# One PSUM tile for both halves of a product, matmuls of 384 columns in the last state step, and another order of the products in the last two groups

## The chip, the cores and the metric

The kernel runs on one core of a Trainium2 chip. A time is the device time of one execution in microseconds. Three executions of the kernel before took 2102.91, 2104.47 and 2105.32 us; their median, 2104.47 us, is the time before. The profile is of one more execution.

Five engines run side by side: TensorE (PE), VectorE (DVE), ScalarE (ACT), GpSimd (POOL) and SyncE (SP, which issues the DMAs). Each takes its own instructions in order, and they wait for one another through semaphores.

## The reference

128 graphs of 128 nodes, each node with 256 features, go through two layers. The first has three steps of message passing with a gated state; the second is an attention over the edges.

```python
# layer 0, h = relu(layernorm(x)); three steps i = 0, 1, 2
m    = einsum('bnd,de->bne', h, weight[i])
aggr = einsum('bst,bsd->btd', A, m)            # A = adj != 0
gi, gh = aggr @ w_ih.T + b_ih, h @ w_hh.T + b_hh   # three gates of 256 each
r, z = sigmoid(i_r + h_r), sigmoid(i_z + h_z)
n    = tanh(i_n + r * h_n)
h    = (1 - z) * n + z * h
# x = x + h
# layer 1, h = relu(layernorm(x))
Wh    = h @ W;  s = Wh.sum(-1)
e     = where(adj == 0, -inf, leaky_relu(s[:, None] + s[None, :], 0.2))
x     = x + softmax(e, -1) @ Wh
```

All values are fp32. Nearly all the arithmetic is in `gi` and `gh`, for the three steps.

## The kernel before, in words

**Groups and steps.** The 128 graphs are worked on in 32 groups of four (G = 4), each with three steps, so there are 96 steps, followed by the group's attention. A table `turns` interleaves the steps of different groups: while one group is in step 0, another is in step 1 and a third in step 2. A step takes about 22 us (the span of 2100.6 us over 96), with its share of the rest.

**The gate products as seven.** The message weights are folded into w_ih, so each step multiplies the state (hT, weights s_hh) and the edge sums (aT, weights s_x0 to s_x2). Both the weights (2x2 blocks of 128) and the columns (two halves of 256) are split in two, and the product of the 2x2 blocks is done with seven block products in place of eight; the sums of halves it needs are hs and gs, made by POOL and DVE. The running sums are called X, Y and Q. In `products` (line 709) the order is: product 1 into X; X is copied to Y (`put`, ACT line 733 or 737 and 739); product 5 into Q; 6 into Y, and Y copied to T2 in SBUF; 7 into Y, Y copied to T3, and Q added to T3 (`add`, DVE line 743); 2 into X; 4 into Y; 3 into Q, and Q added to T2. At the end X, Y, T2 and T3 are the four blocks of the result, and the gates are computed from each.

**PSUM.** Each of X, Y and Q is two tiles: x_rz and x_n and so on, `[P, 2, H]` fp32 with H = 256, which is one bank of 512 values per partition each. [...] T2 and T3 in SBUF are pairs in the same way (t2_rz, t2_n, t3_rz, t3_n).

**Steps 0 and 1** (`gru`) give a transposed result: the weights stand still, and 256 columns of the data stream by. The rz bank holds the gates r and z (four matmuls of 256 columns per product: two gates, state and edges), the n bank holds the state's and the edges' part of n apart (two matmuls of 256). Line 694 issues them.

**Step 2** (`gru_rows`) gives rows, one node per partition: the data stand still, and the weights stream by. Here the rz bank holds r and z for two graphs, filled per product with four matmuls of 256 columns (two graphs, state and edges); the n bank holds the state's and the edges' part of n for both graphs, filled with four matmuls of 128 columns. Line 701 issues them. The biases are laid into X and Q beforehand by a copy on ACT (`seed`, line 726). Per graph pair the gates are one tanh over r and z (ACT line 837, reading the rz bank) and two DVE operations with n (lines 841 and 846, reading the n bank).

**What sets the order.** Each operation is recorded in a `Plan` with an engine, a cost in ns, what it reads and writes (a buffer or a unit range of it), and for the seven products a due time; these form one chain on PE. `Plan.run` then lists all operations in the order in which they would start by these costs, and the instructions are written out in that order, under a scheduler that leaves the order alone. Semaphore waits are put in afterwards, from the order in which instructions touch a tile. Operations on the edges (line 621, bf16), transposes and the attention's products (650, 1077) fill the places between.

**The last two groups** have the same order of the seven products as all others; some of the attention's tiles there take over the banks of x, y and q (`late_bank`).

Of the kernel before, what the change touches and what calls it, by code (L numbers as in the profile page):

```python
# [17 lines left out]
G = 4  # L18
# [197 lines left out]
def kernel(  # L216
# [67 lines left out]
        "w1_sum": (1, "all", const, [P, D]),  # L284
    }
    DTYPE = {"at": I32, "a": BF16, "pl": U16, "plT": U16, "pe": U16, "peT": U16, "p3": BF16}
    phys = {}

    def make(tag, n, kind, pool, shape):
        for s in range(SETS if kind == "set" else 1):  # L290
            for k in range(n):
                phys[tag, s, k] = pool.tile(shape, DTYPE.get(tag, F32), name=f"{tag}_{s}{k}")
# [4 lines left out]
    def ap(b):  # L297
        return phys[(b.tag,) + b.slot]
# [41 lines left out]
    def nat(b):  # L340
        return plain(b)[:, :3 * KD * D].rearrange("p (c e) -> p c e", e=D)

    def turned(src, dst, evict):

        for a in range(2):
            for k in range(KD):
                ps = bank()

                def turn(k=k, a=a, ps=ps):
                    for c in range(3):  # L350
                        nc.tensor.transpose(flat(ps)[:, c * P:(c + 1) * P],
                                            nat(src)[:, 3 * a + c, k * P:(k + 1) * P], ident)
                op("PE", 330, turn, [(src, a, a + 1)], [ps])
                to_sbuf(evict[k % len(evict)], 3 * P, ps, dst[k], 3 * P * a)

# [24 lines left out]
    def weights():  # L380
# [47 lines left out]
        homes = [[buf("h1"), last("hT")] for _ in range(L)]  # L428
        for layer in range(L):
            if layer == 1:  # L430
                turned(w_hh_nat, w_hhT, ("DVE", "ACT"))
                block_sums(w_hhT, W["s_hh"], "POOL", 1000)
            wT, half, msg = uT[layer // 2], layer % 2, w_msg[layer]
            for e in range(KD):
# [38 lines left out]

        def seeds():
            nc.gpsimd.tensor_tensor(plain(tmp[0]), plain(tmp[0]), plain(tmp[1]), OP.add)
            for t, q in ((tmp[0], 0), (tmp[2], 2)):
                nc.gpsimd.tensor_copy(ap(W["seed_x"])[:, q:q + 2, :], halves(t, 0))
                nc.gpsimd.tensor_tensor(ap(W["seed_q"])[:, q:q + 2, :], halves(t, 1), halves(t, 0),
                                        OP.subtract)
        op("POOL", 4000, seeds, tmp, [W["seed_x"], W["seed_q"]] + tmp[:1])  # L480

# [190 lines left out]
    DATA = [None, 0, 2, 3, 7, 4, 6, 5]  # L672
    R, Z, NN = 0, 1, 2

    def product(bank, i, parts, first, rows=False):


        def unit(t, w):
            return (t, DATA[i], DATA[i] + 1) if DATA[i] < 4 else (w, DATA[i] - 4, DATA[i] - 3)

        def source(t, w):
            if DATA[i] < 4:
                return ap(t)[:, DATA[i] // 2, (DATA[i] % 2) * H:(DATA[i] % 2 + 1) * H]
            return ap(w)[:, DATA[i] - 4, :]

        todo = []
        for term in range(max(len(p) for _, p in parts)):
            todo.append([(half, q) + p[term] for half, (q, p) in enumerate(parts) if term < len(p)])
        if len(todo) == 1:
            todo = [[m] for m in todo[0]]  # L690
        for c, chunk in enumerate(todo):
            def mm(c=c, chunk=chunk):
                for m, (half, q, w, t, sums) in enumerate(chunk):
                    nc.tensor.matmul(ap(bank)[:, half, :], ap(w)[:, i - 1, q, :], source(t, sums),  # L694
                                     start=(first and c == 0 and m == 0), stop=False,
                                     skip_group_check=True)

            def mm_rows(chunk=chunk):
                half, q, w, t, sums = chunk[0]
                for m in range(2):  # L700
                    nc.tensor.matmul(  # L701
                        ap(bank)[:, m, half * P:(half + len(chunk)) * P],
                        source(t, sums)[:, m * N:(m + 1) * N],
                        ap(w)[:, i - 1, q:q + len(chunk), :].rearrange("p q m -> p (q m)"),
                        start=False, stop=False, skip_group_check=True)
            plan.cursor += 432 * len(chunk) * SLOT // GATES
            op("PE", 432 * len(chunk), mm_rows if rows else mm,
               [unit(t, s) for _, _, _, t, s in chunk] + [(w, i - 1, i) for _, _, w, _, _ in chunk],
               [bank], due=plan.cursor)

    def products(layer, hT, hs, aT, gs, rows=False):

        five, seven, three, four = (7, 5, 4, 3) if rows else (5, 7, 3, 4)
        state, edges = (W["s_hh"], hT, hs), (W[f"s_x{layer}"], aT, gs)
        kinds = (("rz", ((R, (state, edges)), (Z, (state, edges)))),  # L720
                 ("n", ((NN, (state,)), (NN, (edges,)))))
        X, Y, Q, T2, T3 = ({} for _ in range(5))

        def seed(b, kind, t):
            q = 0 if kind == "rz" else 2
            op("ACT", 590, lambda: nc.scalar.copy(
                ap(b), ap(t)[:, q:q + 2].rearrange("p (o q) m -> p o (q m)", o=1)
                .to_broadcast([P, 2, 2 * P])), [t], [b])

        def put(t, y, bias=None, mark=None):  # L730

            if bias is None or rows:
                op("ACT", 590, lambda: nc.scalar.copy(ap(t), ap(y)), [y], [t], mark=mark)  # L733
                return

            def halves():
                nc.scalar.activation(ap(t)[:, 0], ap(y)[:, 0], AF.Identity,
                                     bias=ap(W["bias_n"])[:, bias:bias + 1])
                nc.scalar.copy(ap(t)[:, 1], ap(y)[:, 1])
            op("ACT", 760, halves, [y, W["bias_n"]], [t], mark=mark)  # L740

        def add(t, q):
            op("DVE", 690, lambda: nc.vector.tensor_tensor(ap(t), ap(t), ap(q), OP.add), [q], [t])  # L743

        for kind, parts in kinds:
            X[kind], Y[kind] = buf("x_" + kind), buf("y_" + kind)
            if rows:
                seed(X[kind], kind, W["seed_x"])
            product(X[kind], 1, parts, not rows, rows=rows)
            put(Y[kind], X[kind], 1 if kind == "n" else None, mark=(plan.group, layer, kind))  # L750
        for kind, parts in kinds:
            Q[kind] = buf("q_" + kind)
            if rows:
                seed(Q[kind], kind, W["seed_q"])
            product(Q[kind], five, parts, not rows, rows=rows)
        for kind, parts in kinds:
            product(Y[kind], 6, parts, False, rows=rows)
            T2[kind] = buf("t2_" + kind)
            put(T2[kind], Y[kind], 2 if kind == "n" else None)
        for kind, parts in kinds:  # L760
            product(Y[kind], seven, parts, False, rows=rows)
            T3[kind] = buf("t3_" + kind)
            put(T3[kind], Y[kind])
            add(T3[kind], Q[kind])
        for kind, parts in kinds:
            product(X[kind], 2, parts, False, rows=rows)
        for kind, parts in kinds:
            product(Y[kind], four, parts, False, rows=rows)
        for kind, parts in kinds:
            product(Q[kind], three, parts, False, rows=rows)  # L770
            add(T2[kind], Q[kind])

        y, t2 = ((0, 1), (1, 0)) if rows else ((1, 0), (0, 1))
        return ((1, 1, T3), (0, 0, X), y + (Y,), t2 + (T2,)), X

# [48 lines left out]
    def gru_rows(layer, hT, hs, aT, gs, rows, x1):  # L826
# [6 lines left out]
        for j, n, src in blocks:  # L833
            i = 2 * n + j
            outs, graphs = slice(j * P, (j + 1) * P), slice(2 * n, 2 * n + 2)
            s_rz, nn = src["rz"], src["n"]
            op("ACT", 700, lambda outs=outs, graphs=graphs, s_rz=s_rz: nc.scalar.activation(
                ap(rz).rearrange("p q (g d) -> p g q d", g=G)[:, graphs, :, outs],
                ap(s_rz).rearrange("p g (q m) -> p g q m", q=2), AF.Tanh, scale=0.5),
               [s_rz], [(rz, i, i + 1), (rz, 4 + i, 5 + i)])  # L840
            op("DVE", 422, lambda outs=outs, graphs=graphs, nn=nn: nc.vector.scalar_tensor_tensor(
                view(u)[:, graphs, outs],
                ap(rz)[:, 0].rearrange("p (g d) -> p g d", g=G)[:, graphs, outs], 1.0,
                ap(nn)[:, :, 0:P], op0=OP.add, op1=OP.mult),
               [nn, (rz, i, i + 1)], [(u, i, i + 1)], two=nn.tag[0] == "t")
            op("DVE", 422, lambda outs=outs, graphs=graphs, nn=nn: nc.vector.scalar_tensor_tensor(
                view(u)[:, graphs, outs], view(u)[:, graphs, outs], 0.5, ap(nn)[:, :, P:2 * P],
                op0=OP.mult, op1=OP.add),
               [nn], [(u, i, i + 1)], two=nn.tag[0] == "t")
        for n in (1, 0):  # L850
            d, lo, hi = buf("d"), 2 * n, 2 * n + 2
            cols = slice(n * GN, (n + 1) * GN)
# [340 lines left out]
```

## Time and profile before

| what | value |
|---|---|
| median of three runs | 2104.47 us |
| the profiled execution | 2102.59 us, its span 2100.6 us |
| PE busy | 2086.8 us, 99% |
| DVE, ACT, POOL busy | 1668.5, 1592.4, 938.0 us |
| clock granted to PE | 1.0 of full |
| first 50 us | PE busy 45.02 us |
| last 21 us | PE busy 15.58 us |
| fp32 matmuls of 256 columns, steps 0 and 1 (line 694) | 2 records each, about 380 ns a record by itself |
| fp32 matmuls of step 2 (line 701) | 256 columns: about 380 ns a record; 128 columns: 275 ns |

[...] What a record costs in a stream is the distance from its start to the next one's start; the timeline shows that. A line of groups gives the operation, its tiles (numbers left out), count, busy time, mean of one, and the idle time of the engine before them with what ended most of it. A line of the timeline gives start, duration, engine, line and operation.

### The profile page before, as it was taken

How to read it: one execution, taken by the hardware profiler on the slowest of the kernel's cores; microseconds unless marked ns; L12 is line 12 of the kernel's file. 1: busy time of each engine (PE TensorE's matmuls, PEld its weight loads, DVE VectorE, ACT ScalarE, POOL GpSimd, SP SyncE). 2: the span in 40 equal slices, each digit the busy share in tenths (PEclk: the TensorE clock that was granted, in tenths of full speed). 3: DMA queues.
4: the chain of work that ended last, by engine and by line, in shares of the span. 5: the costliest groups of instructions: out<-in, count | busy, mean ns of one | idle time of the engine just before them, and what ended most of it. 6: DMA issues, size and time to landing. Idle time of an engine off the chain costs nothing.

```text
span 2100.6 us, 33940 instructions
## 1 busy us (share of the span) xinstructions
PE 2086.8 (99%) x12416; PEld 1862.0 (89%) x12416; DVE 1668.5 (79%) x3370; ACT 1592.4 (76%) x2849; POOL 938.0 (45%) x881
## 2 busy tenths in 40 slices
PE   9999999999999999999999999999999999999998
PEld 6888888898888998898988889988989888988887
DVE  7777888888877888877888778888778887778778
ACT  6577878777878777777778787777777787777676
POOL 5545454345443445544454434455444544335330
PEclk9999999999999999999999999999999999999999
DMA  4323223232233222233222332222322223222331
GB/s 131 61 51 56 53 49 81 61 59 63 69 74 76 57 60 64 68 81 66 52 65 68 73 76 56 61 64 69 80 66 57 60 64 78 56 51 51 76 76 36
DMA packets 365158, 137.21 MB, mean 65 GB/s; under 512 B 296384, under 2 KB 364736, under 8 KB 364992
## 3 DMA queue, kind: packets, MB, share of 16 engines
q1 hardware_dynamic: 364992, 135.05, 28.5%
q8 instruction: 97, 1.59, 0.3%
q14 instruction: 69, 0.57, 0.1%
HBM read 45.36 MB, written 16.78 MB: 30 GB/s over the span
## 4 chain that ended last, share of the span: by engine, by line
PE 97%; DVE 2%; ACT 1%; issue 0%; DMA 0%; DVEq 0%
PE y_rz L694 16%; PE q_rz L694 11%; PE x_rz L694 10%; PE y_n L694 8%; PE y_rz L701 8%; PE misc L621 6%; PE x_n L694 5%; PE q_n L694 5%; PE q_rz L701 5%; PE x_rz L701 5%; PE misc L1077 5%; PE y_n L701 4%; PE x_n L701 3%; PE q_n L701 3%; PE misc L650 2%; PE misc L450 0%
## 5 line engine op out<-in xcount | busy, mean ns | idle before, releaser
L578 POOL TENSOR_TENSOR r<-rows 128x512 f32<-128x512 f32 x126 | 136.1, 1100 | 268.0 <-ACT rows L561 183.4
L733 ACT COPY t_rz<-y_rz 128x512 f32<-128x512 f32 x192 | 112.4, 585 | 178.8 <-PE y_rz L694 89.5
L743 DVE TENSOR_TENSOR t_rz<-t_rz,q_rz 128x512 f32<-128x512 f32 x192 | 131.2, 684 | 98.0 <-ACT t_rz L733 57.0
L603 POOL TENSOR_TENSOR pl<-d,pl 128x512 bf16<-128x512 f32 x64 | 74.7, 1170 | 294.1 <-ACT pl L601 293.9
L694 PE MATMUL y_rz<-hs,s_hh 128*128 128x256 f32 x768 | 197.5, 380 | 0.0
L694 PE MATMUL y_rz<-gs,s_x 128*128 128x256 f32 x768 | 197.1, 379 | 0.0
L668 POOL TENSOR_TENSOR hs<-hT,hs 128x256 f32<-128x256 f32 x96 | 81.8, 852 | 241.6 <-PE q_n L701 173.7
L664 POOL TENSOR_TENSOR hs<-hT 128x512 f32<-128x512 f32 x96 | 130.4, 1358 | 100.4 <-ACT hT L561 32.1
L694 PEld LDWEIGHTS y_rz<-gs,s_x 128*128 128x128 f32 x768 | 145.9, 190 | 19.8
L694 PEld LDWEIGHTS y_rz<-hs,s_hh 128*128 128x128 f32 x768 | 143.1, 190 | 18.8 <-issue 0.5
L581 POOL TENSOR_TENSOR p<-r 128x512 bf16<-128x512 f32 x126 | 153.2, 1235 | 0.0
L743 DVE TENSOR_TENSOR t_n<-t_n,q_n 128x512 f32<-128x512 f32 x192 | 131.2, 683 | 20.5 <-ACT t_n L733 8.2
L694 PE MATMUL x_rz<-hT,s_hh 128*128 128x256 f32 x512 | 131.5, 379 | 0.0
L694 PE MATMUL x_rz<-aT,s_x 128*128 128x256 f32 x512 | 131.4, 379 | 0.0
L624 ACT COPY aT<-misc 128x512 f32<-128x512 f32 x190 | 110.5, 584 | 13.6 <-PE misc L621 9.6
L501 DVE BATCH_NORM_STATS2 st<-rows 128x6 f32<-128x256 f32 x128 | 45.1, 413 | 94.6 <-DMA rows<-in_x_dram 94.5
L816 DVE TENSOR_TENSOR d<-hT,u 128x512 f32<-128x512 f32 x128 | 110.6, 864 | 8.9 <-ACT u L813 8.7
L694 PE MATMUL y_n<-hs,s_hh 128*128 128x256 f32 x384 | 114.4, 379 | 0.0
L694 PE MATMUL y_n<-gs,s_x 128*128 128x256 f32 x384 | 114.2, 379 | 0.0
L598 POOL TENSOR_TENSOR d<-hT,pl 128x512 f32<-128x512 f32 x64 | 90.8, 1421 | 51.4 <-ACT pl L596 45.6
L1077 PE MATMUL misc<-w,uT 128*128 128x256 f32 x480 | 113.3, 380 | 0.3 <-ACT uT L655 0.3
L694 PEld LDWEIGHTS x_rz<-aT,s_x 128*128 128x128 f32 x512 | 97.2, 190 | 13.2
(277 smaller groups left out, 6500.6 us busy)
## 6 DMA issues: line engine op xcount, KB each, us to landing
rows<-in_x_dram SPq DMA_DIRECT2D x32, 512.0 KB, 4.2
x<-in_x_dram SPq DMA_DIRECT2D x32, 512.0 KB, 3.9
out_dram<-x SPq DMA_DIRECT2D x31, 512.0 KB, 2.9
at<-in_adj_dram SPq DMA_DIRECT2D x32, 256.0 KB, 2.8
plT<-pl SPq DMA_TRANSPOSE x186, 3.3
peT<-pe SPq DMA_TRANSPOSE x60, 3.1
e<-in_L_gnn_weight_dram SPq DMA_DIRECT2D x3, 256.0 KB, 3.2
rz<-in_L_gnn_w_ih_dram SPq DMA_DIRECT2D x2, 384.0 KB, 3.9
```

The source lines that it names most:

```text
L578: op("POOL", 1106, lambda part=part: nc.gpsimd.tensor_tensor(ap(r1)[:, part], ap(rows)[:, part], top(rows)[:, part], OP.subtract), [(rows, ...
L581: op("POOL", 1050, lambda part=part: nc.gpsimd.tensor_tensor(ap(p3)[:, part], ap(r1)[:, part], top(r1)[:, part], OP.subtract), [(r1, n, n ...
L598: op("POOL", 1150, lambda k=k, r=r: nc.gpsimd.tensor_tensor(ap(r), ap(hT)[:, k], part(pl, k, 0), OP.subtract), [(hT, 2 * k, 2 * k + 2), (p ...
L621: nc.tensor.matmul(flat(ps)[:, b * N:(b + 1) * N], part(i, b, k), ap(a)[:, b, :], start=(i == 0), stop=(i == 2))
L624: op("ACT", 590, lambda k=k, ps=ps: nc.scalar.copy(ap(dst)[:, k, :], flat(ps)), [ps], [(dst, 2 * k, 2 * k + 2)])
L664: op(eng, cost, lambda: sub(ap(w)[:, 0:2, :], blocks()[:, 1::2, :], blocks()[:, 0:2, :], OP.subtract), [t], [(w, 0, 2)], two=True)
L694: nc.tensor.matmul(ap(bank)[:, half, :], ap(w)[:, i - 1, q, :], source(t, sums), start=(first and c == 0 and m == 0), stop=False, skip_gro ...
L701: nc.tensor.matmul(ap(bank)[:, m, half * P:(half + len(chunk)) * P], source(t, sums)[:, m * N:(m + 1) * N], ap(w)[:, i - 1, q:q + len(chun ...
L733: op("ACT", 590, lambda: nc.scalar.copy(ap(t), ap(y)), [y], [t], mark=mark)
L743: op("DVE", 690, lambda: nc.vector.tensor_tensor(ap(t), ap(t), ap(q), OP.add), [q], [t])
L816: op("DVE", 690, lambda j=j, d=d, cols=cols: nc.vector.tensor_tensor(ap(d), ap(hT)[:, j, :], ap(u)[:, cols], OP.subtract), [(hT, lo, hi), ...
L1077: nc.tensor.matmul(ap(ps)[:, b, :], ap(uT)[:, k, (m + b) * N:(m + b + 1) * N], ap(w1)[:, k, :], start=(k == 0), stop=(k == KD - 1))
```

## The change

It has three parts.

First, `make` cuts the two halves of a pair from one tile: `both["x"]` is `[P, 2, 2, H]`, x_rz is its part 0 and x_n its part 1; likewise y, q, t2 and t3. In PSUM such a tile is two banks.

Second, in step 2 a bank now belongs to a graph. Its four blocks of 128 columns are: the state's part of n, r, z, the edges' part of n. The weights s_hh are laid out as n, r, z (by turning w_hh's blocks in another order), the weights s_x as r, z, n; so the state's product adds into columns 0 to 383 and the edges' product into columns 128 to 511, each with one matmul of 384 columns. The seeds are laid out in the same order. The gates of a graph pair read both banks at once.

Third, in the last two groups product 2 into X and 6 into Y come ahead of 5 and 7, and the gates of X ahead of those of T3.

```diff
     def make(tag, n, kind, pool, shape):
+        name, _, half = tag.partition("_")
+        if shape == [P, 2, H] and half:
+            if half == "rz":
+                both[name] = pool.tile([P, 2, 2, H], F32, name=name)
+            phys[tag, 0, 0] = both[name][:, ("rz", "n").index(half)]
+            return
...
-                turned(w_hh_nat, w_hhT, ("DVE", "ACT"))
+                turned(w_hh_nat, w_hhT, ("DVE", "ACT"), (4, 5, 0, 1, 2, 3))
...
-            def mm_rows(chunk=chunk):
-                half, q, w, t, sums = chunk[0]
-                for m in range(2):
-                    nc.tensor.matmul(
-                        ap(bank)[:, m, half * P:(half + len(chunk)) * P],
-                        source(t, sums)[:, m * N:(m + 1) * N],
-                        ap(w)[:, i - 1, q:q + len(chunk), :].rearrange("p q m -> p (q m)"),
-                        start=False, stop=False, skip_group_check=True)
...
+    def product_rows(bank, i, m, sources):
+        for c, (w, t, sums) in enumerate(sources):
+            plan.cursor += 645 * SLOT // GATES
+            op("PE", 645, lambda c=c, w=w, t=t, sums=sums: nc.tensor.matmul(
+                flat(bank)[:, c * P:(c + 3) * P], source(i, t, sums)[:, m * N:(m + 1) * N],
+                ap(w)[:, i - 1].rearrange("p q m -> p (q m)"), start=False, stop=False,
+                skip_group_check=True), [unit(i, t, sums), (w, i - 1, i)], [bank], due=plan.cursor)
...
-        def seed(b, kind, t):
-            q = 0 if kind == "rz" else 2
-            op("ACT", 590, lambda: nc.scalar.copy(
-                ap(b), ap(t)[:, q:q + 2].rearrange("p (o q) m -> p o (q m)", o=1)
-                .to_broadcast([P, 2, 2 * P])), [t], [b])
+        def seed(b, t):
+            op("ACT", 590, lambda: nc.scalar.copy(flat(b), plain(t)), [t], [b])
...
+        steps = {"Q5": q_five, "Y6": y_six, "Y7": y_seven, "X2": x_two, "Y4": y_four, "Q3": q_three}
+        order = ("Q5 Y6 Y7 X2 Y4 Q3" if plan.group < NG - 2 else "Y6 X2 Q5 Y7 Y4 Q3" if plan.group < NG - 1 else "Y6 X2 Q5 Y7 Y4 Q3").split()
+        for name in order:
+            for kind, parts in kinds:
+                steps[name](kind, parts)
+        x_first = order.index("X2") < order.index("Y7")
...
+            banks_of = [src["rz"], src["n"]]
+            sums = both[src["rz"].tag.split("_")[0]].rearrange("p g a m -> p g (a m)").rearrange(
+                "p g (q m) -> p g q m", q=4)
...
+            op("ACT", 700, lambda outs=outs, graphs=graphs, sums=sums: nc.scalar.activation(
+                ap(rz).rearrange("p q (g d) -> p g q d", g=G)[:, graphs, :, outs], sums[:, :, 1:3, :],
+                AF.Tanh, scale=0.5), banks_of, [(rz, i, i + 1), (rz, 4 + i, 5 + i)])
```

In the changed kernel the matmuls of steps 0 and 1 are at line 703, those of step 2 at line 717, the copies at 744 (seed), 749, 753 and 755, the add at 759, the tanh of the gates at 818 and 836 (steps 0 and 1) and 869 (step 2).

## The prediction

> **What bounds the kernel now.** I read the page first: share of each engine, then the chain that ended last.
>
> ```profile
> PE 2086.8 (99%) x12416; PEld 1862.0 (89%) x12416; DVE 1668.5 (79%) x3370; ACT 1592.4 (76%) x2849; POOL 938.0 (45%) x881
> ...
> PE 97%; DVE 2%; ACT 1%; issue 0%; DMA 0%; DVEq 0%
> ```
>
> TensorE is busy for 99% of the span and carries 97% of the chain. Since a busy PE need not be a PE at its peak, I next read the timeline in a steady stretch, for the distance between the starts of its groups:
>
> ```profile
> 1025.61 0.61 PE L701 MATMUL q_n<-s_hh,hs 128*128 128x128 f32 x4
> 1026.05 0.61 PE L701 MATMUL q_n<-s_x,gs 128*128 128x128 f32 x4
> 1026.50 1.03 PE L701 MATMUL y_rz<-s_hh,hs 128*128 128x256 f32 x4
> 1027.37 1.03 PE L701 MATMUL y_rz<-s_x,gs 128*128 128x256 f32 x4
> 1028.23 0.61 PE L701 MATMUL y_n<-s_hh,hs 128*128 128x128 f32 x4
> ```
>
> One fp32 matmul is two records here. Four records of 256 columns take 0.865 us from start to start (216 ns each), four of 128 columns 0.445 us (112 ns). Neither a reader nor a weight load opens a gap. Why none does is seen at one of the few places where PE stops, in the last 60 us, where its queue runs short:
>
> ```profile
> 2056.44 1.03 PE L701 MATMUL x_rz<-s_x,aT 128*128 128x256 f32 x4
> ...
> 2057.50 0.57 ACT L733 COPY y_rz<-x_rz 128x512 f32<-128x512 f32 x1 [0.73 <-PE x_rz L701]
> ...
> 2057.98 0.60 ACT L726 COPY q_rz<-seed_q 128x512 f32<-128x512 f32 x1
> ...
> 2058.63 1.13 PE L701 MATMUL q_rz<-s_hh,hs 128*128 128x256 f32 x4 [0.28 <-ACT q_rz L726]
> ```
>
> The last x_rz record has streamed in at 2056.44+0.865=2057.30. ACT starts 0.20 us later; PE starts 0.05 us after ACT's copy ends (2058.58), and its first group then takes 1.13 instead of 1.03 us. So a reader that PE must wait for, with no other PE work between, costs 0.20 + the reader's time + 0.05 + 0.10 us. The readers' times, from the groups by shape:
>
> ```profile
> L733 ACT COPY t_rz<-y_rz 128x512 f32<-128x512 f32 x192 | 112.4, 585 | 178.8 <-PE y_rz L694 89.5 <-PE y_rz L701 89.1
> L789 ACT ACTIVATE rz<-x_rz,bias_s 128x256 f32<-128x256 f32 x64 | 29.8, 466 | 12.5 <-PE x_rz L694 12.2
> L743 DVE TENSOR_TENSOR t_rz<-t_rz,q_rz 128x512 f32<-128x512 f32 x192 | 131.2, 684 | 98.0 <-ACT t_rz L733 57.0 <-PE q_rz L694 24.6 <-PE q_rz L701 16.2
> ```
>
> A full round trip is therefore 0.93 us for a copy, 0.82 us for a gate's tanh, 1.03 us for an add. Today it is hidden: while ACT copies y_rz, PE works on the n half, which is another tile, for 0.86 us or more, and often on an attention product as well.
>
> **What the Trainium skill says.** "TensorE: Matmul & The Clock Gate", section Back-to-back issue gap, gives a streaming time proportional to the columns plus about 2.5 ns per matmul. The trace agrees: 216 ns at 256 columns is 2.7 ns above 256/1.2, and 112 ns at 128 columns is 5 ns above. "Perfetto Trace Analysis", section Matmuls, asks that independent groups rotate through different banks so that the evacuation of one overlaps the next; the 0.86 us of n work above is that overlap. "PSUM — Partial Sum Buffer", section PSUM bank collisions raise a hardware error, says that accesses of two engines must be kept apart within a bank, reads included, and that different banks run clean. So the chip asks for no wait between the rz and the n bank, and the profile of before shows ACT reading y_rz (2063.34 to 2063.93) while PE writes y_n (2063.08 to 2063.97).
>
> **The change, part by part.** (1) *Wide products of the last step.* Per product and group 4 matmuls of 256 columns and 4 of 128 become 4 of 384. In records: 8x216 + 8x112 = 2.624 us before. A 384-column record is not in the trace; between the 256-column records here (216) and 512-column ones of the weight preparation (line 450, 429 ns from start to start) it is 322.5 ns, so 8x322.5 = 2.580 us. Gain 0.044 us, times 7 products and 32 groups: **-9.9 us**. Its bounds are -13 us (no fixed part at all: 8x320) and 0.
>
> (2) *Order of PE's queue.* Blocks of bf16 edge products stand together more often. After such a block the first fp32 matmul costs some 55 ns (the group at 1002.43 takes 0.92 us to the next start, elsewhere 0.865). The built queue has 116 such changes, it had 157: **-2.3 us**.
>
> (3) *Seeds, copies, adds and gates.* The built programs have the same number of instructions of the same sizes on ACT, DVE, POOL and SP. The reordered transposes of w_hh and the seed layout cost nothing new. DMAs are the same, in nearly the same places.
>
> (4) *One tile for two halves.* Here is the cost. `make` now cuts x_rz and x_n (also y, q, t2, t3) out of one tile. In the built program the waits go by that tile: an instruction on one half waits for the last earlier one of another engine on either half. PE's queue of the changed kernel, with the semaphores waited for:
>
> ```
> L703 Matmult y_134<-hs_00_85,s_hh_00_157 128x256 [waits Activation_49]
> L703 Matmult y_134<-hs_00_85,s_hh_00_157 128x256
> L703 Matmult y_134<-gs_00_89,s_x0_00_158 128x256 x2
> L703 Matmult y_134<-hs_00_85,s_hh_00_157 128x256
> L703 Matmult y_134<-gs_00_89,s_x0_00_158 128x256 [waits Activation_49]
> ```
>
> The first four write the rz bank, the last two the n bank. I followed each awaited value to the instruction that raises it. ACT's copy of the rz bank stands, in the written order, between the two n matmuls. So the copy waits for the first n matmul, although it doesn't read its bank, and the second n matmul waits for the copy. Between those two nothing stands in PE's in-order queue: a full round trip. In the wide step the same happens between the two matmuls of the second graph.
>
> I counted in the built program, over the seven products of all 96 steps, each PE wait on ACT or DVE, and the PE work (by the periods above) between the matmul that lets the reader go and the matmul that waits for it. Nothing lies between in 164 cases with a copy, 60 with a tanh, 58 with an add, and 14 with the n copy in two pieces (0.46+0.37+0.35 = 1.17 us). Sum: 164x0.93 + 60x0.82 + 58x1.03 + 14x1.17 = 152.5+49.2+59.7+16.4 = **+278 us**. In 75 more, part is covered; the uncovered rest is **+20 us**. The same count over the program of before gives 7 cases and 1.7 us, which fits the few stops its trace shows.
>
> Behind a waiting matmul stands all of PE's queue, so each stop moves everything. The readers can be late themselves: of 192 rz copies, 97+58 were waited for by ACT, so 19% found ACT late; of the 96 last adds of rz, 36+27 were waited for by DVE, so 34% found it late. One more instruction of 0.6 to 0.7 us ahead of these: 224x0.19x0.6 + 58x0.34x0.7 = 39 us. As a slower PE leaves ACT and DVE more room, I take half, **+20 us**; bounds 0 and +39.
>
> (5) *Waits between ACT and DVE.* A gate's tanh on one bank and DVE's product on the other now also take turns. The hidden state they make is used a step or more (about 20 us) later, and POOL, which needs it next, idles for half the span. I take 0; if that cover were gone, about 0.4 us for each of some 200 gate blocks would be +80 us.
>
> (6) *Other order of the products in the last two groups.* In 2040 to 2060 us PE stands still for 1.8 us, which is the most that an earlier X2 can return; against that the attention of the last group shares tiles too, with some four added round trips. Together **+3 us**, bounds -2 and +6.
>
> Sum against the profiled execution: 2102.6 (span 2100.6 and 2.0 around it) - 9.9 - 2.3 + 278 + 20 + 20 + 3 = 2411.4. The median of the runs lies 1.9 us above the profiled execution: **2413 us**, 14.7% more.
>
> **The rivals.** *A, waits as counted*, 2413 us: 0.76. Its own range comes from the round trip: 0.1 us less on 296 cases is -30 us. The tail of the profile has such a case (a transpose at 2087.68, which waits for a 256-column copy of 0.37 us, starts 0.74 us after the one before; less that one's own 0.11 it is 0.63, where my constants give 0.72). With 0.1 us more, or all readers late as before, it is some 30 us more. With the unknown terms, 2360 to 2470.
>
> *B, the readers queue as well*: every second round trip meets a busy ACT or DVE and the turns of (5) reach PE: 148x0.6 + 80 = +170 us on A, 2580 us: 0.12. For it: ACT at 76% and DVE at 79%. Against: a slower PE leaves them idle more.
>
> *C, half the round trips overlap with stops that come anyway*: PE's stops delay all, so a later reader may already be done. 278 halves: 2275 us: 0.08. Against: each counted wait begins at a matmul that stands just ahead of it, so an earlier stop doesn't help it.
>
> *D, the other side*: the waits find their readers done and only (1), (2) and (6) act: 2104.5 - 9 = 2095 us, faster: 0.04. It decides at the second n matmul: it holds if at least 0.93 us of other PE work stands ahead of it, as the 0.86 us and more stand in the kernel before. In the built queue 0 us stands there; only a program other than the built one would make D true. The wide products not being wide is excluded, as the queue shows 896 matmuls of 384 columns.
>
> **How the numbers follow.** A is the likeliest, 2413 us. From 2330 to 2500 lies nearly all of A and the near ends of B and C, about 8 in 10. This kernel's runs spread over 0.1%, so a difference of 0.2% is about what can be told from none. Slower: A, B and C, 0.96; faster: D less a part, 0.03; same: 0.01.
>
> **What the profile after would show.** PE's share falls to about 86% with its busy time near 2080 us. The waits list PE's x, y, q matmuls (lines 703 and 717) behind ACT line 749 (about 180 times, 0.8 us each), ACT line 818 (60) and DVE line 759 (60), led by ACT 749 with 130 to 150 us; the chain passes through ACT and DVE for more than 10%. 384-column records stand 322 ns apart. It would be wrong if PE stays at 99%, or if the waits are far from 300 in number; if the number is right and the mean is 0.6 or 1.2 us, only the round trip was mis-sized.

## The result, and the profile after

The changed kernel takes **2401.64 us** (median of four runs, 2398.76 to 2403.47), the kernel before 2104.0 us beside it. The ratio is **1.1413, 95% interval 1.1393 to 1.1433**: 14% slower. The forecast was 2413 us, with a range of 2330 to 2500. The profiled execution took 2403.47 us, its span is 2401.6 us.

From the page of the changed kernel, the busy times and the chain that ended last:

```profile
PE 2167.3 (90%) x10624; PEld 1641.3 (68%) x10624; DVE 1697.1 (71%) x3370; ACT 1609.2 (67%) x2849; POOL 927.1 (39%) x881
...
PE 23%; ACT 2%; DVE 2%; issue 1%; DMA 0%; SPq 0%; DVEq 0%; ACTq 0%
```

TensorE was busy for 99% of the span and now is for 90%. No other engine has come near its limit: DVE and ACT have lower shares than before. The chain's shares add up to 28% only: here it breaks off, so it says nothing of the rest. The list of PE's waits does (total us, number, longest us):

```profile
PE y L703 <- ACT t L749: 48.1, 69, 0.7
PE y L717 <- ACT t L749: 39.0, 56, 1.2
PE q L703 <- DVE t L759: 37.0, 46, 1.7
PE x L703 <- ACT y L749: 23.1, 34, 0.7
PE y L703 <- ACT rz L818: 19.3, 34, 0.7
PE y L703 <- ACT t L755: 16.1, 23, 1.1
PE x L703 <- ACT rz L818: 13.6, 24, 0.6
PE q L717 <- DVE t L759: 10.3, 13, 0.9
PE x L717 <- ACT y L749: 5.7, 8, 0.7
```

In the kernel before, the longest entry of this list for a product was

```profile
PE y_rz L701 <- ACT t_rz L733: 2.8, 2, 1.5
```

Now there are hundreds of short ones. The copies at line 749 stop PE 170 times (69 + 56 + 34 + 8, and 3 in a line not shown), the adds at 759 stop it 59 times.

What one such stop looks like is seen in the timeline of the changed kernel, here at an add:

```profile
1025.90 0.59 PE L703 MATMUL q<-hT,s_hh 128*128 128x256 f32 x2
...
1026.53 0.69 DVE L759 TENSOR_TENSOR t<-t,q 128x512 f32<-128x512 f32 x1 [0.78 <-PE q L703]
...
1027.27 0.70 PE L703 MATMUL q<-aT,s_x 128*128 128x256 f32 x2 [0.78 <-DVE t L759]
...
1028.01 0.69 DVE L759 TENSOR_TENSOR t<-t,q 128x512 f32<-128x512 f32 x1 [0.79 <-PE q L703]
```

The first n matmul has streamed in at 1025.90 + 2x0.216 = 1026.33. DVE starts its add of the *rz* half 0.20 us later and ends at 1027.22; the second n matmul starts 0.05 us after that. The add of the n half, which does need this matmul, follows at 1028.01. So between 1025.90 and 1027.27 PE has done 0.43 us of work and has stood for 0.94 us. In the wide step it is the same with the second graph's bank:

```profile
1041.75 0.81 PE L717 MATMUL y<-s_hh,hs 128*128 128x384 f32 x2
1042.59 0.58 ACT L749 COPY t<-y 128x512 f32<-128x512 f32 x1 [2.53 <-PE y L717]
...
1043.23 0.91 PE L717 MATMUL y<-s_x,gs 128*128 128x384 f32 x2 [0.67 <-ACT t L749]
1043.98 0.49 PE L717 MATMUL x<-s_hh,hT 128*128 128x384 f32 x1
```

The waiting time in brackets is shorter than the loss. PE stands from 1042.40 (1041.75 + 2x0.323) to 1043.23, 0.83 us, and the first group takes 0.75 us to the next start where two records of 384 columns take 0.65. The loss is 0.93 us; the bracket shows 0.67. It starts only at 1042.56, where the last record's listed time ends, 0.16 us after the next record could have started, and it leaves out the 0.10 us by which the first group is longer.

For the sums below I took the distance from each PE record's start to the next one's, over the whole trace, less the regular distance of that kind of record (112, 216, 323 ns for 128, 256, 384 columns). What is left over is delay (the regular distances are medians in whole ns, so each sum is good to one or two us):

| PE, us | before | after |
|---|---|---|
| sum of the regular distances | 2072.3 | 2063.3 |
| sum of the delays | 23.0 | 332.9 |

So the wide products bring 9.0 us and the delays take 309.9 us, together +300.9, which is the difference of the two profiled executions (2403.47 - 2102.59 = 300.9).

### The profile page after: what moved, and what is told of

Same layout as the page of the kernel before. It is cut to its first block, busy times and chain, and to the rows that moved or that the text cites. A ratio compares the mean times of both kernels' runs of the same rounds, so it can differ in the third digit from the quotient of the medians.

```text
span 2401.6 us, 30231 instructions
## 1 busy us (share of the span) xinstructions
PE 2167.3 (90%) x10624; PEld 1641.3 (68%) x10624; DVE 1697.1 (71%) x3370; ACT 1609.2 (67%) x2849; POOL 927.1 (39%) x881
## 3 DMA queue, kind: packets, MB, share of 16 engines
q8 instruction: 83, 1.36, 0.2%
## 5 line engine op out<-in xcount | busy, mean ns | idle before, releaser
L759 DVE TENSOR_TENSOR t<-t,q 128x512 f32<-128x512 f32 x384 | 259.2, 686 | 266.7 <-ACT t L749 150.9
L703 PE MATMUL y<-gs,s_x 128*128 128x256 f32 x1152 | 323.5, 390 | 78.2 <-ACT t L749 48.1
L749 ACT COPY t<-y 128x512 f32<-128x512 f32 x320 | 184.2, 586 | 310.4 <-PE y L703 179.7
L703 PE MATMUL y<-hs,s_hh 128*128 128x256 f32 x1152 | 314.6, 382 | 5.9 <-ACT t L755 5.4
L703 PEld LDWEIGHTS y<-gs,s_x 128*128 128x128 f32 x1152 | 209.5, 190 | 148.3 <-ACT t L749 75.8
L703 PE MATMUL x<-aT,s_x 128*128 128x256 f32 x768 | 213.8, 387 | 37.8 <-ACT y L749 23.1
L703 PEld LDWEIGHTS y<-hs,s_hh 128*128 128x128 f32 x1152 | 216.0, 190 | 37.9 <-ACT t L755 7.9
L703 PE MATMUL x<-hT,s_hh 128*128 128x256 f32 x768 | 207.8, 379 | 0.0
L703 PEld LDWEIGHTS x<-aT,s_x 128*128 128x128 f32 x768 | 141.0, 190 | 78.2 <-ACT y L749 36.5
L703 PEld LDWEIGHTS x<-hT,s_hh 128*128 128x128 f32 x768 | 145.8, 190 | 25.9
```

The lines of the kernel that those rows point to most:

```text
L703: nc.tensor.matmul(ap(bank)[:, half, :], ap(w)[:, i - 1, gate, :], source(i, t, sums), start=(first and c == 0 and m == 0), stop=False, sk ...
```

## The experiments

**The shared tile alone.** Theory A says that the loss comes from the tile being one for two halves, as the waits go by the tile. Then the kernel before must lose as much when only its `make` is changed, with the old products, seeds, gates and order:

```diff
     def make(tag, n, kind, pool, shape):
+        name, _, half = tag.partition("_")
+        if name in ("x", "y", "q", "t2", "t3") and shape == [P, 2, H] and half:
+            if half == "rz":
+                both[name] = pool.tile([P, 2, 2, H], F32, name=name)
+            phys[tag, 0, 0] = both[name][:, ("rz", "n").index(half)]
+            return
```

> The kernel before with one edit: make cuts each pair (x, y, q, t2, t3) from one tile; matmuls, order and gates are those of before. Theory A (waits by the shared tile): its built program has 387 product matmuls that wait for an ACT or DVE reader with no PE work between (190 behind copies, 82 behind adds, 107 to 114 behind a tanh, where before there is none), and some 75 partly covered: 0.942 us per copy, 1.047 per add, 0.83 per tanh as measured in the changed kernel, together about +385 us: 2490 us, slower than the changed kernel itself. Rival (the wide products or the order of the products make the time): no change, 2104 us. Rival (about half of the waits is hidden in a program with the old matmuls): about 2290 us.

Measured: 2514.18 us, ratio 1.1947 (1.1925 to 1.1968). Shared tiles without a single wide product lose 410 us, even more than the whole change. The expected sum was 24 us short. The chain that ended last is whole here and passes through DVE for 15% and ACT for 10%.

The same edit with a shorter list tells which tiles do it. Only Q, `name in ("q",)`:

> The kernel before with q_rz and q_n alone from one tile. Theory A: 85 waits behind an add (82) or a seed (3) with nothing between, 1.047 us each: +89 us, 2193 us. Rival: no change, 2104 us. If the stops add to each other the sum of parts would not hold and it would be below 2160 us.

Measured: 2198.36 us, ratio 1.0446 (1.0427 to 1.0465). The two lines of PE's waits behind the add of rz:

```profile
PE q L700 <- DVE t_rz L749: 46.0, 55, 2.7
PE q L707 <- DVE t_rz L749: 22.0, 28, 0.9
```

One tile, 83 waits, 94 us. And only the tiles in SBUF, `name in ("t2", "t3")`:

> The kernel before with the SBUF pairs t2 and t3 alone each from one tile. Theory A: the product matmuls wait as before (7 partly covered, 1.7 us), because matmuls never touch these tiles; only ACT and DVE wait for each other on them. 2104 us within 0.3%. Rival (the shared SBUF tiles cost too, through late readers): some tens of us more, 2120 to 2180 us.

Measured: 2103.77 us, ratio 1.0 (0.9991 to 1.0009). T2 and T3 are written and read by ACT and DVE alone, and what these wait for each other doesn't reach the time. It is the pairs of PSUM tiles that cost: Q's 94 us by itself; the rest of the 410 us is left for the pairs of X and Y, which were not shared one by one.

**The readers planned later.** A rival to the waits would be that something in the two-bank tiles themselves is slow. If it is the waits, the tiles can stay as they are: it is enough that the planner puts a reader of PE's results later, so that more PE work stands between. In the changed kernel:

```diff
-    LAG = {"PE": 250, "ACT": 300, "DVE": 300, "POOL": 300, "SP": 4000}
+    LAG = {"PE": 1200, "ACT": 300, "DVE": 300, "POOL": 300, "SP": 4000}
```

> The changed kernel, tiles shared as there, with one number altered: the recording layer reckons a reader 1200 ns after its matmul instead of 250 (LAG of PE), so ACT's and DVE's readers are written later in the order, mostly behind the second matmul of the other half. Same instructions. Theory A (the round trip exists where the reader is written between the two matmuls of the other half): 65 full round trips are left in place of 296 (57 behind copies, 4 behind the n copy in two pieces, 3 longer chains) and some 65 partly covered: +84 us against no waits; 2104 - 10 - 2 + 84 = 2176 us. Rival (sharing a tile costs the same whatever the order, or wide products are slow): about 2400 us.

Measured: 2193.07 us, ratio 1.042 (1.0406 to 1.0434). One number of the planner returns 209 of the 298 us, with the same tiles and the same instructions. The expected 2176 us was 17 short. The delays fall from 332.9 to 120.2 us. What stays is mostly the wide step; the longest entries of PE's waits are:

```profile
PE y L717 <- ACT t L749: 40.2, 57, 2.1
PE y L703 <- ACT t L755: 9.4, 5, 3.3
PE y L703 <- ACT y L755: 3.9, 4, 1.0
```

**The wide products with tiles apart.** The other way round: the changed kernel with x, y and q as two tiles each again (`name in ("t2", "t3")` in its `make`). A gate that reads both banks then has to be split by bank where X and Y are read in the wide step, which adds 64 instructions on ACT and 128 on DVE:

```diff
-        if shape == [P, 2, H] and half:
+        if name in ("t2", "t3") and half:
...
+            if src["rz"].tag[0] != "t":
+                pair = [(2 * n + m, src[kind]) for m, kind in enumerate(("rz", "n"))]
+                for g1, bk in pair:
+                    op("ACT", 470, lambda outs=outs, g1=g1, bk=bk: nc.scalar.activation(
+                        ap(rz)[:, :, g1 * D + outs.start:g1 * D + outs.stop],
+                        flat(bk)[:, P:3 * P].rearrange("p (q m) -> p q m", q=2), AF.Tanh, scale=0.5),
+                       [bk], [(rz, i, i + 1), (rz, 4 + i, 5 + i)])
+                for g1, bk in pair:
+                    op("DVE", 290, lambda outs=outs, g1=g1, bk=bk: nc.vector.scalar_tensor_tensor(
+                        view(u)[:, g1, outs], ap(rz)[:, 0, g1 * D + outs.start:g1 * D + outs.stop], 1.0,
+                        flat(bk)[:, 0:P], op0=OP.add, op1=OP.mult), [bk, (rz, i, i + 1)], [(u, i, i + 1)])
...
+                continue
```

> The changed kernel with x, y and q as two tiles each, as before (t2 and t3 stay shared); as one instruction can't read two tiles, the tanh over X and Y in the last step becomes two of 256 elements, and the two DVE operations four of 128 (64 more on ACT, 128 more on DVE). Wide products and the other order stay. Theory A: no full round trip is left (4 partly covered, 0.5 us), the wide products give 9.9 us and 40 fewer changes from bf16 to fp32 2.2 us: 2092 us, 0.6% faster than before. Rival (the wide products themselves are slow, or ACT and DVE become late with the split gates): 2104 us or more.

Measured: 2111.42 us, ratio 1.0033 (1.0021 to 1.0044). The 300 us are gone, so theory A stands. But the gain of 9 us did not appear, and the expected 2092 us was missed by 19. By the distances between records the products do bring 8.6 us (regular sum 2063.7), while the delays are 38.4 us against 23.0: -8.6 + 15.4 = +6.8 us, which is the measured ratio. So there are new stops, of another kind. (The 8.6 and the 9.0 us above differ by no more than the rounding of the distances.)

**The order alone, and the wide products in the old order.** The kernel before with the new order of products in the last two groups:

```diff
+        order = ("Q5 Y6 Y7 X2 Y4 Q3" if plan.group < NG - 2 else "Y6 X2 Q5 Y7 Y4 Q3").split()
```

> The kernel before with the third part of the change alone: in the last two groups products 6 and 2 come ahead of 5 and 7, and the gates of X ahead of those of T3. Prediction's term: -3 to +3 us, within 0.2% of 2104 us. Rival (it shortens the end as the stops at 2040 to 2060 us suggest): -2 us, which 5 rounds may just show.

Measured: 2103.09 us, ratio 0.9996 (0.9988 to 1.0004): no difference that can be told. And wide_apart with `order = "Q5 Y6 Y7 X2 Y4 Q3".split()` in all groups:

> The run wide_apart (two tiles per pair, wide products, split gates) with the old order of the products in the last two groups too. wide_apart took 2111.4 us where 2092 was expected; its trace shows some 13 stops of 0.6 to 2.5 us at product matmuls whose reader on ACT was late because ACT stood behind DVE (an exponential waiting for DVE's scores) in its queue. Theory (an accident of the written order; it moves with any change of it): another time between 2092 and 2112 us, with other stops. Rival (the new order itself costs these 15 us): 2094 us and no stops over 0.6 us between 200 and 2000 us.

Measured: 2108.83 us, ratio 1.002 (1.0013 to 1.0027). The delays are again 38.4 us. The new order isn't what makes the new stops.

**Where the new stops come from.** The largest one of wide_apart, in its timeline:

```profile
919.45 1.41 DVE L509 BATCH_NORM_STATS2 st<-rows 128x6 f32<-128x256 f32 x4 [3.35 <-DMA rows<-in_x_dram]
920.13 2.49 POOL L586 TENSOR_TENSOR r<-rows 128x512 f32<-128x512 f32 x2 [10.05 <-ACT rows L569]
...
921.75 1.41 DVE L1078 TENSOR_TENSOR e<-e,s 128x512 f32<-128x512 f32 x1
922.58 2.93 POOL L589 TENSOR_TENSOR p<-r 128x512 bf16<-128x512 f32 x2
923.20 1.41 DVE L1080 SCALAR_TENSOR_TENSOR e<-e 128x512 f32<-128x512 f32 x1
925.37 0.17 DVE L1084 TENSOR_SCALAR low<-top 128x4 f32<-128x4 f32 x1
925.57 1.27 ACT L1089 ACTIVATE e<-e,low 128x128 f32<-128x128 f32 x4 [4.39 <-DVE low L1084]
926.75 0.56 ACT L749 COPY t<-y_rz 128x512 f32<-128x512 f32 x1
...
927.46 1.10 PE L703 MATMUL y_rz<-hs,s_hh 128*128 128x256 f32 x4 [2.21 <-ACT t L749]
```

Read from the bottom: PE waits for a T copy; the copy stands on ACT behind the attention's exponentials; these waited 4.39 us for DVE; and there two passes over the scores took 1.41 us each, while POOL was at work. Ahead of the passes, in the same queue, a statistics instruction had waited 3.35 us for a DMA (the first line). Three ways to cut this were tried.

First, DVE's results planned later in wide_apart (`"DVE": 300` to `700`):

> The run wide_apart with one number altered: the recording layer reckons an instruction that needs DVE's result 700 ns later instead of 300 (LAG of DVE), so ACT's queue has other work ahead of such instructions. Same instructions. Theory (late readers behind DVE make the stops): the stops of 0.6 to 2.5 us mostly go, 2092 to 2100 us, faster than before. Rival (the split gates load ACT and DVE too much, or wide products are slow by themselves): 2108 to 2115 us as wide_apart.

Measured: 2111.28 us, ratio 1.0029 (1.0018 to 1.0041). Missed. The delays in the middle of the span fell from 23.7 to 17.1 us, but those in its last 70 us rose from 7.3 to 12.3; all together they are 39.1 us against 38.4.

Second, the exponentials on ACT held behind the step's two T2 copies, in both orders:

```diff
-            put(T2[kind], Y[kind], 2 if kind == "n" else None)
+            put(T2[kind], Y[kind], 2 if kind == "n" else None, mark=(plan.group, layer, "t2_" + kind))
...
-           [e, den] if ending else [e], turn=(g + 2, 1, "rz"))
+           [e, den] if ending else [e], turn=(g + 2, 1, "t2_n"))
```

> wide_apart_old_order, with one thing moved: the attention's exponentials on ACT are held behind the step's two T2 copies instead of behind the first y copy. Theory N (in the kernel with separate tiles the stops of PE come from T2 and T3 copies that stand on ACT behind attention work): only two of its 21 stops have exponentials within 4 us ahead, 2.4 us of 17.2, so 2106 us, ratio 1.001. If exponentials were behind most of the stops: 2095 us, ratio 0.996.

> wide_apart with the same move. Here more of the stops have the exponentials ahead of the late copy (4.39 us of ACT's idle time before them in the largest). If they are the cause, the 18.5 us of stops fall below half and the time is 2100 to 2104 us, ratio 0.998 to 1.000; if the copies then stand behind the next attention copies (lines 1197, 1201) instead, 2108 to 2112 us.

Measured: 2110.53 us (1.0028, 1.0016 to 1.0039) and 2110.82 us (1.0033, 1.0022 to 1.0044). No help: the stops of over 0.15 us in the middle of the span stay near 18 us in both. But the move didn't reach the late copies, so these two runs don't tell whether the exponentials matter. The late copy of the largest stop is that of T3 (926.75 in wide_apart), which comes after those of T2 (918.24 to 920.65), and the exponentials stood between the two already. In apart_new_turn they stand directly ahead of the late copy as before:

```profile
926.96 1.28 ACT L1090 ACTIVATE e<-e,low 128x128 f32<-128x128 f32 x4 [4.39 <-DVE low L1085]
928.15 0.56 ACT L749 COPY t<-y_rz 128x512 f32<-128x512 f32 x1
```

In the old order, too, six stops have them directly ahead of the late copy and two more have them a copy or two ahead, not two in all as the expectation has it.

Third, the passes on DVE themselves. In wide_apart 28 of the 60 overlap a POOL instruction and take 1.36 us in the mean, and the other 32 take 0.69 us; in the kernel before it is 4 of 60. The Trainium skill ("SBUF — State Buffer", section Who interferes with whom) says that a DVE instruction with two SBUF inputs contends with a GpSimd instruction that reads SBUF, and calls the port pair that they share an exclusive lock, so that the one that comes second waits. These two passes have two inputs in SBUF, POOL's residuals at 586 and 589 read SBUF, and the doubled time (1.41 us where the overlap is long, 0.69 without) agrees. The planner knows of this and never plans the two together, but it counts 691 ns for a pass, and in the run they meet all the same; which of the two comes off its planned time was not traced. So I gave the plan a longer pass, to part them:

```diff
-            op("DVE", cost, lambda: nc.vector.tensor_tensor(es(), es(), wide(s), OP.add), [s], [e],
+            op("DVE", cost + 300, lambda: nc.vector.tensor_tensor(es(), es(), wide(s), OP.add), [s], [e],
...
-            op("DVE", cost, lambda: nc.vector.scalar_tensor_tensor(
+            op("DVE", cost + 300, lambda: nc.vector.scalar_tensor_tensor(
```

> wide_apart_old_order, where the planner is told 300 ns more for each of the two passes over the attention's scores on DVE. Theory S: with the wide step these passes meet POOL's residual work (25 of 60 passes overlap a POOL instruction and take 1.39 us, the others 0.69 us; in the kernel before 4 of 60), which makes DVE, POOL and then ACT late and gives the new stops. If the longer plan parts them (under 10 of 60 overlap), the stops fall below half: 2098 to 2102 us, ratio 0.997 to 0.999. If they overlap as often: 2107 to 2111 us and nothing is told. If they are parted and the stops stay, S falls.

> wide_apart with the same 300 ns. Theory S: 28 of 60 passes overlap POOL's work there (1.36 us against 0.69). If fewer than 10 do, 2098 to 2104 us, ratio 0.997 to 1.000; if as many, 2109 to 2113 us.

Measured: 2104.51 us (1.0, 0.9991 to 1.0008) in the old order, which misses its 2102 by 2.5 us, and 2102.98 us (0.9996, 0.9987 to 1.0005) in the new one, as expected. The passes by shape, one of the kernel before, then both in wide_apart and in apart_new_scores (count, busy us, mean ns):

```profile
L1033 DVE TENSOR_TENSOR e<-e,s 128x512 f32<-128x512 f32 x30 | 21.6, 719 | 0.9
```

```profile
L1078 DVE TENSOR_TENSOR e<-e,s 128x512 f32<-128x512 f32 x30 | 30.3, 1009 | 0.9
L1080 DVE SCALAR_TENSOR_TENSOR e<-e 128x512 f32<-128x512 f32 x30 | 29.9, 998 | 0.7
```

```profile
L1078 DVE TENSOR_TENSOR e<-e,s 128x512 f32<-128x512 f32 x30 | 23.5, 783 | 0.7
L1080 DVE SCALAR_TENSOR_TENSOR e<-e 128x512 f32<-128x512 f32 x30 | 21.0, 702 | 0.2
```

Now 7 of 60 overlap by more than 0.1 us (6 in the old order). The stops of over 0.15 us in the middle of the span fall from 18.5 to 11.0 us (old order: 17.2 to 7.7), and the time, by the ratios, by 7.8 us (4.2). That they fall below half holds in the old order only.

But this run took away two things at once. With the longer plan the passes also stand ahead of the statistics that wait for the DMA (at 909.89 and 911.53, the statistics at 923.26). In wide_apart there are eleven groups between 500 and 1760 us in which both passes are doubled. In six of them the statistics just ahead had waited for the DMA, and each of the six has a stop of PE behind it:

| PE's stop at, us | 543.88 | 927.46 | 1120.50 | 1312.93 | 1505.26 | 1697.51 |
|---|---|---|---|---|---|---|
| DVE had waited for the DMA | 2.17 | 3.35 | 2.58 | 1.97 | 1.87 | 1.80 |
| delay of PE | 1.16 | 2.38 | 1.32 | 0.72 | 0.61 | 0.54 |

```profile
1112.76 1.41 DVE L509 BATCH_NORM_STATS2 st<-rows 128x6 f32<-128x256 f32 x4 [2.58 <-DMA rows<-in_x_dram]
...
1120.50 1.10 PE L703 MATMUL y_rz<-hs,s_hh 128*128 128x256 f32 x4 [1.16 <-ACT t L749]
...
1689.78 1.41 DVE L509 BATCH_NORM_STATS2 st<-rows 128x6 f32<-128x256 f32 x4 [1.80 <-DMA rows<-in_x_dram]
...
1697.51 1.10 PE L703 MATMUL y_rz<-hs,s_hh 128*128 128x256 f32 x4 [0.38 <-ACT t L749]
```

The other five (986.63, 1179.69, 1372.15, 1564.53, 1757.76) have no such wait, and no stop of PE over 0.3 us in the 13 us after. In the last four columns the delay is the DMA wait less 1.26 us. So doubled passes alone make no stop here; what PE's delay follows is DVE's wait for the DMA. An estimate from these numbers: with passes of 0.69 us, which take 1.44 us less for the two, only the wait of 3.35 us would still have stopped PE. The six stops are 6.7 of the 18.5 us and are gone in apart_new_scores. So the collision with POOL and the wait for the DMA together made them; no run parts the two, and what made the other stops is open.

The account closes here too: -8.6 us from the products, delays of 31.9 against 23.0 us, together +0.3 us, and the measurement finds no difference. This version is 12.4% faster than the changed kernel, and no faster than the kernel before.

## Why the prediction was right

Its step (4), one tile for two halves, carries it. The runs show it from three sides: the tiles alone lose as much (shared_all), the tiles taken apart lose it no more (wide_apart), and other work put between the writer and the waiter returns two thirds of it (after_late_readers). Each term against the distances in the traces:

| term | predicted, us | in the trace, us |
|---|---|---|
| (1) wide products | -9.9 | -9.0 |
| (4) 164 waits on a copy | 152.5 (0.93 each) | 157.9 (0.96) |
| (4) 60 on a tanh | 49.2 (0.82) | 50.0 (0.83) |
| (4) 58 on an add | 59.7 (1.03) | 62.4 (1.08) |
| (4) 14 on the n copy in two pieces | 16.4 (1.17) | 15.3 (1.09) |
| (4) partly covered | 20 | 26 |
| (4) readers that are late | 20 | at most 8, within the lines above |
| (2) changes from bf16 to fp32 | -2.3 | -2.3 |
| (5) ACT and DVE by turns | 0 | none to be seen |
| (6) order | 3 | none to be told, without shared tiles (order_alone: 0.9996) |

All 296 waits that were counted in the built program did stop PE, so rival D (readers done in time) and C (half of them overlapped with other stops) are out. The round trip read from one stop at the end of the trace of before was right within 5% for copy, tanh and add, and 7% too long for the n copy in two pieces.

The oversized term is **late readers**: the mean of the 296 is 0.965 us, and that of the predicted trips 0.94. The surplus of 285.6 - 277.8 = 7.8 us is all that lateness and mis-sizing of the trip have cost. The step's bound of 0 was the better guess: it said itself that a slower PE leaves the readers more room. For the same reason rival B, readers that queue, got nothing; DVE's share fell from 79% to 71%, ACT's from 76% to 67%. Part of the closeness is luck: late readers were put 12 us too high, the partly covered waits 6 us too low.

In (1) the 384-column record came out as foreseen: half of them take 322 ns and half 323. The slip is in the 128-column record: the prediction's own 0.445 us for four are 111 ns each, not 112, as the trace's mean of 111.4 also says. On 1792 records 0.6 ns are 1.1 us. Term (2) came out as well: an fp32 record follows a bf16 one in 158 places before and in 117 after, and at the median such place the distance is 56 ns longer; 41x0.056 = 2.3 us. For (5), the delays after, without the 285.6 us of full round trips and the 26 us of partly covered ones, are 21.3 us, no more than the 23.0 us of before.

One reading of the prediction is looser than it sounds. What the Trainium skill ("TensorE: Matmul & The Clock Gate", section Back-to-back issue gap) gives at full clock is columns/2.4 + 2.5 ns, which makes 109 ns for 256 columns. A record here takes 216 ns. Only the form agrees, a part that goes with the columns and a small fixed one; the slope of 1/1.2 ns per column is this trace's own ((322.5 - 216)/128 = 0.83).

The foretold 322 ns of the 384-column records came true; three other signs were misread ahead. PE's share is 90% and its busy time 2167 us, not 86% and 2080 us: each stop leaves 0.164 us of a record's listed time (0.380, less the 0.216 to the next start) with no next record over it, and the first records after it are longer by 0.10 us. 296x0.264 = 78 us more of busy time, which is nearly the whole excess of 87. By the same 0.264 us, a wait in the list is shorter than what it costs: the 170 at line 749 stand there with 117.6 us, 0.69 each, where 0.8 each and 130 to 150 us had been foretold. And the chain was to pass through ACT and DVE for more than 10%: it breaks off at 28% and shows nothing; in shared_all it is whole and shows 25%.

What stays open: why wide_apart has the passes so late (around 920 us of the span they start at 921.75 and 923.20, behind the wait for the DMA and beside POOL's residuals from 920.13 on; in the kernel before they start at 907.99 and 909.38 and the residuals at 921.25; what moved them was not tried), what each of the two conditions is worth, and whether a plan exists in which the 8.6 us come home.

## What to carry to other kernels

In these programs waits go by the tile, so banks that are to be filled and emptied in turns need a tile each; a view of both costs a round trip of about 0.95 us at every turn when nothing else stands between in PE's queue. Such a loss can be counted before a run: list each wait of the bounding engine, the work between the instruction that frees the reader and the one that waits for it, and price what isn't covered with one stop read from the trace. When a reader is late, follow its engine's queue back past the slow instruction to the last wait: a DMA that lands late far ahead can be what is passed on. And when an experiment moves an instruction, see in its trace that it stands elsewhere. A gain of a few tenths of a per cent on a kernel at 99% is at the mercy of the schedule: it has to be looked for in the distances between records, and the new stops beside it.

## What was not expected of the hardware

- Two DVE passes over 128x512 fp32 with both inputs in SBUF take 0.69 us by themselves and 1.36 to 1.39 us in the mean where a POOL instruction overlaps them (28 of 60 in wide_apart, 25 in wide_apart_old_order). Their mean in the group list (1009 ns against 719 in the kernel before) is the place where it shows first.
- The list of waits understates a short stop of PE: 0.67 us listed at 1043.23, 0.93 us lost. For stops of about a microsecond the busy share hides a quarter.
- A tile over two PSUM banks isn't slow in itself: the 256-column records keep 216 ns, and with the readers planned later most of the loss is gone.
